# Half of the guard to GpSimd, and the second norm's end one unit later, in a four-layer decoder

## The chip, the core and the metric

The kernel runs on one core of a Trainium2 chip. The core has five engines that work through their own instruction queues in order and meet only at semaphores: TensorE (PE in the profile, with PEld for its weight loads), VectorE (DVE), ScalarE (ACT), GpSimd (POOL) and SyncE (SP), which here issues most of the transfers. The metric is the device time of one execution in microseconds (us). Less is better.

## The reference, cut to what matters

The program is a decoder of four layers on 128 sequences of 64 positions and 128 channels. Each layer has self-attention, attention to a context of the same size, and a feed-forward part. The change touches one part alone, the second layer's attention to the context (`L1_xattn`):

```python
x = x + _L1_xattn_ref(ctx_1024, _layernorm(x, axis=-1), ...)

def _L1_xattn_ref(encoded, decoded, Wq, bq, Wk, bk, Wv, bv, gamma, beta):
    # q from decoded, k and v from encoded; 16 heads of 8 channels
    qk = jnp.einsum('bhqd,bhkd->bhqk', q, k)
    qk = jnp.where(jnp.isnan(qk), -jnp.inf, qk)
    attn = jax.nn.softmax(qk, axis=-1)
    attn = jnp.where(jnp.isnan(attn), 0.0, attn)
    v = jnp.where(jnp.isnan(v), 0.0, v)
    z = jnp.einsum('bhqk,bhkd->bhqd', attn, v)
    z = z.reshape(B, Sq, D)
    x = z + decoded
    mu = jnp.mean(x, axis=-1, keepdims=True)
    var = jnp.var(x, axis=-1, keepdims=True)
    return (x - mu) * jax.lax.rsqrt(var + LN_EPS) * gamma + beta
```

So there is a first norm (of x, before the attention) and a second norm (of attention plus the normed x), scaled by gamma, shifted by beta and then added to x. The weights that are not a number become zero: the kernel does that by a maximum with 0, which it calls the guard.

## The kernel before, in words

The activations `x` stay in the core's memory as 64 tiles of 128 rows. Four tiles make a **group** (512 rows), so there are 16 groups. An attention part goes through its groups in halves of two tiles, called **units**; unit u belongs to group u // 2. `chain` (from L251 on) writes the order of all work of a layer's attention parts out by hand: the second layer's chain has 32 groups, 16 of the self-attention and then 16 of the attention to the context, and each engine executes its instructions in the order in which `chain` emits them.

In unit u the chain emits, in this order: the hooks of place "a"; `maxima` of unit u + 1 (scores in PE, four DVE reductions, L555, and five small POOL instructions that split the maxima into three bf16 pieces, L561 to L565); the second `mix` of the unit before (PE, L671 and L680); `divide` of the unit before (ACT's logarithm and exponential, L700 and L701, and three DVE instructions, L703 to L707); the first `weights` (PE L613 and L622, then four ACT exponentials into the tile p, L648). Then an odd unit finishes the group before (PE L913, ACT L917, transfers L920), projects a later group's keys and queries (L454, L459) and measures x of a group four ahead (DVE L205 and L206, then `ve` and `rs` on POOL, L208 and L210). An even unit computes values (PE L488, DVE L502 and L503, ACT L511) and turns an input (L432, L440). Then come the first guard of the unit (L656), the hooks of place "b", the second `weights`, the first `mix`, the turning of the maxima (PE L573, DVE L577), the second guard, in an even unit the scaling of the first norm of a group three ahead (`norm_act`: two POOL instructions for `nb`, L218 and L219, and four ACT activations, L221), and the hooks of place "c".

A `mix` can't begin before the guard of its weights: it multiplies the values by p, whose first 512 columns and last 512 columns are two halves of the tile, and it needs both from its first few matmuls on.

The second norm runs in hooks, counted in units from a group's own first unit: `load` (even, "b" of unit 4) fetches z from memory by SP, L890; `add` (odd, "a" of unit 5) adds the normed x on POOL, L895; `measure` (odd, "b" of unit 5) computes the statistics on DVE and POOL; `last` (even, "c" of unit 6) calls `normed_add`, which scales z by `norm_act` and then emits three POOL instructions on 128x512: times gamma (L874), plus beta (L875), and x plus z (L877). z has two buffers.

Behind the chain the second layer's feed-forward part begins. Its first input needs the x that the last L877 writes.

Of the kernel before, what the change touches and what calls it, by code (L numbers as in the profile page):

```python
# [53 lines left out]
def bc(ap, axis, n):  # L54

    v = ap.unsqueeze(axis)
    shape = list(v.shape)
    shape[axis] = n
    return v.broadcast_to(shape)


class Decoder:
# [163 lines left out]
    def norm(self, dst, src, stats=None):  # L226
        mv, rs = self.stats(src) if stats is None else stats
        for i in range(G):
            self.nc.vector.tensor_scalar(  # L229
                out=dst[:, i, :], in0=src[:, i, :], scalar1=mv[:, i, 0:1],  # L230
                scalar2=rs[:, i : i + 1], op0=ALU.subtract, op1=ALU.mult,
            )
# [419 lines left out]
    def guard(self, q, i):  # L652
        if q["kind"] == "guarded":

            for p in q["p", i]:
                self.nc.vector.tensor_scalar_max(p, p, 0.0)  # L656

    def mix(self, u, i, q):

# [209 lines left out]
    def normed_add(self, q, gamma, beta):  # L869

        nc, g, z = self.nc, q["g"], q["z"]
        norm = self.norm_act if q.get("norm") == "act" else self.norm
        norm(z, z, q["z_stats"])
        nc.gpsimd.tensor_tensor(out=z, in0=z, in1=bc(gamma, 1, G), op=ALU.mult)  # L874
        nc.gpsimd.tensor_tensor(out=z, in0=z, in1=bc(beta, 1, G), op=ALU.add)  # L875
        xg = self.x[:, g * G : (g + 1) * G, :]
        nc.gpsimd.tensor_tensor(out=xg, in0=xg, in1=z, op=ALU.add)  # L877

    def l1_xattn(self, wp):
        nc = self.nc  # L880
        w = self.qkvo(["L1_xattn_WqT", "L1_xattn_WkT", "L1_xattn_WvT"], wp)


        heads = self.dram.tile([self.nt * 2, H, S * HD], F32, name="l1x_heads")
        rows = heads.rearrange("s h (r d) -> (s h r) d", d=P)

        def load(q):
            g = q["g"]
            q["z"] = self.zp.tile([P, G, P], F32, tag="z", name="z")
            nc.sync.dma_start(  # L890
                out=q["z"], in_=rows[g * W : (g + 1) * W, :].rearrange("(t p) d -> p t d", p=P)
            )

        def add(q):
            nc.gpsimd.tensor_tensor(out=q["z"], in0=q["z"], in1=q["xn"], op=ALU.add)  # L895

        def measure(q):
            q["z_stats"] = self.stats(q["z"])

        def last(q):  # L900
            self.normed_add(q, self.spread["L1_xattn_gamma"], self.spread["L1_xattn_beta"])

        def finish(q, cxT):
            g = q["g"]

            zh = self.zh[q["n"] % 2]
            for r in range(2):
                ps = self.place().rearrange("p (d q) -> p d q", d=4)
                for d in range(4):

                    cols = self.consts[:, 4 * r + d : 4 * r + d + P : 4]
                    for i in range(G):
                        nc.tensor.matmul(  # L913
                            ps[i * 32 : (i + 1) * 32, d, :], lhsT=cols,
                            rhs=cxT[:, i * P : (i + 1) * P], start=True, stop=True,
                        )
                nc.scalar.copy(zh[:, :, 4 * r : 4 * r + 4], ps.rearrange("h d q -> h q d"))  # L917
            for i in range(G):
                k = 2 * (g * G + i)
                nc.sync.dma_start(  # L920
                    out=heads[k : k + 2].rearrange("s h n -> h s n"),
                    in_=zh[i * 32 : (i + 1) * 32 : 2].rearrange("h (s q) d -> h s (q d)", s=2),
                )

        return dict(
            hooks={
                ("b", 4): load, ("a", 5): add, ("b", 5): measure, ("c", 6): last,
            },
            w=w, source="ctx", finish=finish, bq=self.vec["L1_xattn_bq"],
            bk=self.vec["L1_xattn_bk"], bv3=self.row3["L1_xattn_bv"], kind="guarded", scale=1.0,  # L930
            norm="act",
        )
# [1300 lines left out]
```

## Time and profile before

| What | us |
|---|---|
| median of three runs | 3945.98 (3937.51 to 3946.89) |
| the profiled execution's own time | 3928.93 |
| its span, from the first to the last instruction | 3926.8 |
| PE busy in the span | 3279.9 (84%) |
| DVE busy | 2639.9 (67%) |
| ACT busy | 1924.3 (49%) |
| POOL busy | 1918.9 (49%) |
| L656 on DVE, 128 instructions, first and last start | 1263.5 and 1571.8 |
| L874, L875 and L877 on POOL in this part, each | 1.26 to 1.45 |

The span has many stages with different limits, so the shares above are averages. The stage of the change is a stretch of 309 us, 1263.5 to 1572.8, of which PE is busy 263.4, DVE 246.4, ACT 198.3 and POOL 154.4 us. In a line of the trace in order of time the first number is the start in us from the span's start, the second the duration (of several alike, from the first's start to the last's end), then follow engine, line, operation, output and inputs, shapes and count; in brackets stands the idle time before it and who ended it. A line of waits names who waited, for whom, how long in total, how often, and the longest.

### The profile page before, as it was taken

Reading aid. Unit: us, or ns where it says so; the run is one execution under the profiler, and the core shown is the slowest. Engines: PE = TensorE matmul, PEld = TensorE weight load, DVE = VectorE, ACT = ScalarE, POOL = GpSimd, SP = SyncE. Lnnn points to the kernel's source line nnn. Section 1 sums busy time; section 2 is a strip of 40 time slices with the busy share of each in tenths; the row PEclk is TensorE's granted clock in tenths of the full one; section 3 lists DMA queues with packets and bytes.
Section 4 is the critical chain, followed back from the end, with each engine's and each line's share of the span. In section 5 each row is a group of like instructions: output and inputs, shape, how many; then the busy total and the mean of one; then the engine's idle time right before and its main releaser. Section 6 shows DMA issues by size and latency. Waiting matters only on the chain.

```text
span 3926.8 us, 174155 instructions
## 1 busy us (share of the span) xinstructions
PE 3279.9 (84%) x76225; PEld 2164.2 (55%) x76237; DVE 2639.9 (67%) x7604; ACT 1924.3 (49%) x4720; POOL 1918.9 (49%) x3087
## 2 busy tenths in 40 slices
PE   5999996645999888467999998498896998799898
PEld 4666663323666666234666775244444666566566
DVE  6776675644887788696667766344435677898675
ACT  3566773103555666585556664122233555456422
POOL 3334664685442455684223434267775436863221
PEclk9999997656999999558999998699998999999999
DMA  3222222443111221000112222133333211111111
GB/s 99 65 65 79 85 95 58 101 90 70 58 55 42 64 68 57 22 1 29 53 56 71 102 93 59 37 63 74 72 65 76 69 54 52 42 44 56 54 46 36
DMA packets 246815, 243.20 MB, mean 62 GB/s; under 512 B 58459, under 2 KB 166883, under 8 KB 246054
## 3 DMA queue, kind: packets, MB, share of 16 engines
q1 hardware_dynamic: 137014, 165.24, 12.9%
q0 software_dynamic: 35264, 29.54, 5.2%
q10 hardware_dynamic: 73776, 37.27, 3.3%
q8 instruction: 599, 9.81, 1.1%
q14 instruction: 162, 1.33, 0.1%
HBM read 97.57 MB, written 63.04 MB: 41 GB/s over the span
## 4 chain that ended last, share of the span: by engine, by line
PE 57%; DVE 18%; POOL 10%; issue 6%; ACT 5%; DMA 4%; SPq 1%; another core or an unknown queue 0%; ACTq 0%; POOLq 0%; DVEq 0%
PE ps L613 6%; PE ps L540 6%; PE po L671 6%; PE po L680 5%; PE ps L454 4%; DVE m L555 3%; PE ps L722 3%; PE ps L2055 2%; PE ps L488 2%; PE pg L2036 2%; PE pu L2040 2%; DVE xn L229 2%; POOL rs L210 2%; PE ps L432 1%; DVE sb L549 1%
## 5 line engine op out<-in xcount | busy, mean ns | idle before, releaser
L648 ACT ACTIVATE p<-ps 128x256 f32<-128x256 f32 x2048 | 620.2, 391 | 152.7 <-PE ps L622 143.8
L555 DVE TENSOR_REDUCE m<-ps 128x8 f32<-128x512 f32 x896 | 555.9, 682 | 185.4 <-PE ps L540 183.0
L561 POOL CAST mx<-m 128x32 bf16<-128x32 f32 x256 | 56.0, 219 | 920.0 <-DVE m L555 919.6
L671 PE MATMUL po<-p,vx 128*32 128x64 f32 x18432 | 411.9, 224 | 86.8 <-DVE p L656 40.7
L613 PE MATMUL ps<-qx,kT 32*64 32x128 f32 x18432 | 430.3, 283 | 15.0 <-issue 9.2
L671 PEld LDWEIGHTS po<-p,vx 128*32 128x32 f32 x18432 | 302.4, 110 | 243.0 <-issue 116.4
L613 PEld LDWEIGHTS ps<-qx,kT 32*64 32x64 f32 x18432 | 277.7, 132 | 178.8 <-issue 99.9
L1287 POOL DMA_INDIRECT l_rows_y<-y,l_idx x192 | 306.5, 1596 | 130.2 <-DVE y L2071 57.1
L680 PE MATMUL po<-p,consts 128*32 128x128 f32 x8192 | 341.4, 276 | 9.5 <-issue 9.0
L540 PE MATMUL ps<-kx,qT 32*64 32x256 f32 x8192 | 308.6, 393 | 7.9 <-DMA kx<-kT 4.1
L700 ACT ACTIVATE r<-po 128x256 f32<-128x256 f32 x224 | 85.8, 383 | 416.5 <-PE po L680 407.1
L1280 POOL DMA_INDIRECT xe<-l_rows_n,l_idx x192 | 204.8, 1066 | 124.1 <-issue 40.6
L210 POOL TENSOR_TENSOR rs<-ve,neghalf 128x4 f32<-128x4 f32 x240 | 252.0, 1050 | 19.9
L577 DVE COPY mT<-ps 128x256 bf16<-128x256 bf16 x256 | 73.3, 286 | 243.6 <-PE ps L573 242.8
L680 PEld LDWEIGHTS po<-p,consts 128*32 128x32 f32 x8192 | 221.1, 111 | 16.4 <-issue 15.4
L540 PEld LDWEIGHTS ps<-kx,qT 32*64 32x64 f32 x8192 | 162.4, 133 | 83.3 <-issue 40.5
L208 POOL TENSOR_SCALAR ve<-mv 128x4 f32<-128x4 f32 x240 | 57.5, 240 | 308.3 <-DVE mv L206 294.1
L206 DVE BATCH_NORM_AGGREGATE mv<-st 128x2 f32<-128x6 f32 x960 | 172.5, 181 | 31.2
L205 DVE BATCH_NORM_STATS2 st<-x 128x6 f32<-128x128 f32 x704 | 186.7, 265 | 4.3 <-POOL x L329 4.0
L2045 DVE SCALAR_TENSOR_TENSOR hT<-pu,ub,sg 128x512 f32<-128x512 f32 x128 | 95.8, 750 | 138.3 <-PE pu L2040 101.0
L622 PE MATMUL ps<-mT,pick 32*64 32x128 bf16 x8192 | 179.2, 216 | 9.4 <-issue 9.4
L511 ACT COPY vx<-ps 64x512 f32<-64x512 f32 x256 | 149.0, 582 | 29.4 <-PE ps L488 15.2
(398 smaller groups left out, 7496.9 us busy)
## 6 DMA issues: line engine op xcount, KB each, us to landing
qx<-qT SPq DMA_DIRECT2D x560, 64.0 KB
kx<-kT SPq DMA_DIRECT2D x512, 64.0 KB
l_rows_y<-zeros SPq DMA_DIRECT2D x64, 256.0 KB
cT<-in_ctxT SPq DMA_DIRECT2D x64, 256.0 KB
fed<-l_rows_y ACTq DMA_DIRECT2D x64, 256.0 KB
l_rows_n<-fn ACTq DMA_DIRECT2D x32, 256.0 KB
l_turned<-fT ACTq DMA_DIRECT2D x32, 256.0 KB
s_xT<-l_turned SPq DMA_DIRECT2D x32, 256.0 KB
```

The source lines that it names most:

```text
L205: nc.vector.bn_stats(st[:, i, :], src[:, i, :])
L206: nc.vector.bn_aggr(mv[:, i, :], st[:, i, :])
L210: nc.gpsimd.tensor_tensor(out=rs, in0=ve, in1=self.neghalf, op=ALU.pow)
L540: nc.tensor.matmul(ps[r][s * S : (s + 1) * S, i * 256 : (i + 1) * 256], lhsT=qT[f, k], rhs=kx[f, :, k], start=mask != "causal", stop=mask ...
L555: nc.vector.tensor_reduce(m[:, :, r, :], ps[r].rearrange("p (t h k) -> p t h k", t=2, k=S), AX.X, ALU.max)
L613: nc.tensor.matmul(heads(r, o)[:, :, s, :], lhsT=kT[f, k], rhs=qx[f, o:4:2, k], start=s == 0 and mask is None, stop=s == 1 and not softmax,)
L622: nc.tensor.matmul(st[r][o * S : (o + 1) * S, j * P : (j + 1) * P], lhsT=self.pick[f, 2 * j + o, :], rhs=q["mT"][f, i, :], start=False, st ...
L648: nc.scalar.activation(p[:, 2 * r : 2 * r + 2], st[r], AF.Exp, scale=1.0 if mask == "bias" else scale)
L671: nc.tensor.matmul(po[e * 32 : (e + 1) * 32, 0, i, s * S : (s + 1) * S], lhsT=vx[:, k, j, :], rhs=p[j // 4][:, j % 4, s * S : (s + 1) * S] ...
L680: nc.tensor.matmul(po[e * 32 : (e + 1) * 32, 1, i, :], lhsT=self.spread_sum[:, jp, :], rhs=p[e // 2][:, (2 * e + jp) % 4, :], start=jp == ...
L1280: self.nc.gpsimd.indirect_dma_start(out=dst, out_offset=None, in_=table, in_offset=bass.IndirectOffsetOnAxis(ap=idx, axis=0), bounds_check ...
L1287: self.nc.gpsimd.indirect_dma_start(out=table, out_offset=bass.IndirectOffsetOnAxis(ap=idx, axis=0), in_=src, in_offset=None, bounds_check ...
```

## The change

Two things change, both in the second layer's attention to the context. First, of each guard's two instructions the second goes to GpSimd: the first 512 columns of p are guarded on VectorE, the last 512 on GpSimd. Second, `normed_add` no longer calls `norm_act` where that is the norm; a hook `scale` does so at the old place ("c" of unit 6), and the rest, times gamma, plus beta and the addition to x, is emitted by a hook `later` in "b" of unit 7. The hooks of a place are emitted for the older group first, so `later` of one group stands ahead of `measure` of the next. The last of the 16 groups keeps the old place for all of it. The reach of the hooks, `far` in the chain, becomes 7.

```diff
     def guard(self, q, i):
         if q["kind"] == "guarded":
 
-            for p in q["p", i]:
-                self.nc.vector.tensor_scalar_max(p, p, 0.0)
+            for engine, p in zip((self.nc.vector, self.nc.gpsimd), q["p", i]):
+                engine.tensor_scalar_max(p, p, 0.0)
...
     def normed_add(self, q, gamma, beta):
 
         nc, g, z = self.nc, q["g"], q["z"]
-        norm = self.norm_act if q.get("norm") == "act" else self.norm
-        norm(z, z, q["z_stats"])
+        if q.get("norm") != "act":
+            self.norm(z, z, q["z_stats"])
         nc.gpsimd.tensor_tensor(out=z, in0=z, in1=bc(gamma, 1, G), op=ALU.mult)
...
         def measure(q):
             q["z_stats"] = self.stats(q["z"])
+
+        def scale(q):
+            self.norm_act(q["z"], q["z"], q["z_stats"])
+            if q["g"] == self.ng - 1:
+                last(q)
+
+        def later(q):
+            if q["g"] < self.ng - 1:
+                last(q)
 
         def last(q):
             self.normed_add(q, self.spread["L1_xattn_gamma"], self.spread["L1_xattn_beta"])
...
             hooks={
-                ("b", 4): load, ("a", 5): add, ("b", 5): measure, ("c", 6): last,
+                ("b", 4): load, ("a", 5): add, ("b", 5): measure, ("c", 6): scale, ("b", 7): later,
             },
```

## The prediction

> **What bounds the kernel now.** I began with the page's first lines, to see how large the stage is that the change touches.
>
> ```profile
> span 3926.8 us, 174155 instructions
> ...
> L1140 POOL TENSOR_SCALAR hq<-h x64: 1917/1918/1982, 1621.4 to 1798.7; 128x512 bf16<-128x512 f32 x64
> ...
> L1382 POOL TENSOR_SCALAR ex<-ex x16: 404/404/458, 370.4 to 651.4; 128x256 f32<-128x256 f32 x16
> ...
> L656 DVE TENSOR_SCALAR p<-p x128: 392/420/1497, 1263.5 to 1571.8; 128x512 f32<-128x512 f32 x128
> ```
>
> The last three lines come from asking for single source lines (shortest, median, longest ns). The guard runs from 1263.5 to 1572 us, so only 309 us of the span change, and the tail behind them. Next, the engines' busy time by stretch: us, then PE, PEld, DVE, ACT, POOL busy.
>
> ```profile
> 1267.00:1323.80 56.80, 52.13 (x1754) 37.58 (x1750) 46.35 (x116) 38.43 (x100) 17.08 (x47) 1.00 0.21 64
> 1323.80:1511.20 187.40, 157.12 (x5034) 111.40 (x5027) 149.27 (x379) 119.62 (x317) 101.28 (x198) 0.96 0.22 67
> ```
>
> The first stretch holds three groups, before any second norm's scale and addition runs; the second holds nine with it: 18.9 us against 20.8 us for a group (two units). Nothing is full in the second, PE 84%, DVE 80%. So a circle of waits sets the pace. The waits on PE in that stretch:
>
> ```profile
> PE po L671 <- DVE p L656: 27.7, 25, 3.2
> PEld po L671 <- DVE p L656: 39.2, 51, 3.3
> ```
>
> PE waits for the guard. Then one 20.0 us group in order of time, engine by engine.
>
> ```profile
> 1405.61 1.65 ACT L221 ACTIVATE xn<-x,nb,rs 128x128 f32<-128x128 f32 x4
> 1407.16 1.63 ACT L221 ACTIVATE z<-z,nb,rs 128x128 f32<-128x128 f32 x4
> 1408.70 0.45 ACT L700 ACTIVATE r<-po,tiny 128x256 f32<-128x256 f32 x1
> ...
> 1411.73 1.27 POOL L877 TENSOR_TENSOR x<-x,z 128x512 f32<-128x512 f32 x1
> 1412.96 1.45 POOL L895 TENSOR_TENSOR z<-z,xn 128x512 f32<-128x512 f32 x1
> 1414.36 0.40 POOL L561 CAST mx<-m 128x32 bf16<-128x32 f32 x1
> ...
> 1416.06 0.23 POOL L208 TENSOR_SCALAR ve<-mv 128x4 f32<-128x4 f32 x1
> ...
> 1412.39 0.18 DVE L206 BATCH_NORM_AGGREGATE mv<-st 128x2 f32<-128x6 f32 x1
> 1412.49 2.20 DVE L656 TENSOR_SCALAR p<-p 128x512 f32<-128x512 f32 x2
> 1416.56 0.75 DVE L656 TENSOR_SCALAR p<-p 128x512 f32<-128x512 f32 x2
> ...
> 1414.74 0.58 PE L671 MATMUL po<-p,vx 128*32 128x64 f32 x26 [1.10 <-DVE p L656]
> 1416.03 0.28 PE L573 MATMUL ps<-identh,mx 128*128 128x128 bf16 x2 [0.21 <-POOL mx L565]
> 1417.29 0.66 PE L671 MATMUL po<-p,vx 128*32 128x64 f32 x30
> ```
>
> The three additions of the previous group (L874, L875, L877, 4.1 us, waiting for ACT's scale) and L895 stand on POOL ahead of the maxima's pieces (L561 to L565). They also lie beside the odd unit's first guard, which takes 2.20 us for two instructions, where it takes 0.75 us at 1416.56. Two marks divide the group: **t**, DVE's end of measuring x in the odd unit (1412.57), and **s**, the start of PE's second mix of that unit (1417.29). Now t to s is 4.72 us, and s to the next t 15.28 us (1397.29 to 1412.57).
>
> **The change, part by part.** *Removed from DVE:* 64 of 128 guards. Undisturbed they cost 0.39 us, so 1.5 us of DVE a group.
>
> *Added to POOL:* 64 guards of a form that the trace doesn't hold (128x512, f32 in place, max). L1382 takes 404 ns for 256 columns and L219 238 ns for 4, thus 0.66 ns a column, and 0.58 us for 512. L1140 has the full size, and a min, but a bf16 output and two operations: 1.92 us. These are the ends. The GPSIMD Engine Reference, section 3.1, gives 769 ns for 512 elements of a tight loop; by that, an estimate, I would add 51 us below instead of 42. I take 0.58 us, since L1382 is nearer in kind (f32 to f32 with a scalar), and keep 1.92 us for the range.
>
> *Moved:* the three POOL additions go from the end of the even unit to the odd unit, behind its first guard and ahead of its second. They carry no DMA. `scale` keeps its place (four ACT activations, two POOL multiplications for nb). SP's load of z into the buffer that they free (L890, issued at 1422.1) comes some 9.5 us after t, and they now end near t+6.5: no wait on SP, and nothing behind it. POOL's order in the odd unit becomes L895, the maxima's pieces, ve and rs of x, half a guard, three additions, ve and rs of z, half a guard.
>
> *From t to s, new.* ve and rs follow the measuring, beside DVE's half guard; at 1309.05 the same pair ended 1.8 us later. Half guard 0.65 with its gap; three additions 4.1 (1408.88 to 1413.00); ve and rs of z 1.4 (1416.06 to 1417.38, with the gap); half guard 0.65. Sum **8.6 us**, against 4.72. PE could be there at t+4.8 (1.8 + 0.65 to start the first mix, then 2.34 of mix, turning and maxima: 1414.74 to 1417.29 less its 0.21 wait). So the second half guard holds PE for 3.8 us. DVE's own half is done by then, even if an addition delays it: late without cost.
>
> *From s to the next t, new.* DVE's reductions are over when PE starts, so the division starts when ACT has r, at s+2.15 instead of s+2.53, and the even unit gains 0.45 us up to ACT's weights (ready at s+7.85, not 8.3). POOL's half guard ends at s+8.5. Behind it now stand the nb multiplications, which before were done at 1402.4; xn starts at s+9.0 instead of 8.32, z follows, and L700 starts at s+12.1 instead of 11.41. Then r 0.95, division 1.35, measuring 1.65: the next t at s+**16.1**. The maxima's pieces no longer stand behind the additions, which saves PE's 0.21 us wait and the doubled guard; both are in these figures. All in all 24.7 us a group against 20.8: **+3.9**, nine times **+35**.
>
> *The last four groups* measure no x and, after the first, scale no xn. Without these, r is ready near s+11.5, p(U) at 12.7, and 0.65 + 4.1 + 1.4 + 0.65 make 19.5 us a group. The gaps between ACT's L700 of the even units are 18.5, 17.8, 19.0, then 7.0 us for the last odd unit; I get 19.5, 19.5, 19.5 and 10.2: **+6.5**.
>
> *The first three groups* have no additions. The odd unit's half guard waits for ve and rs (t+2.45 instead of t+0.73); PE loses about 1.5 us, the even unit gives 0.2 back: **+4**.
>
> *The tail.* After PE's last mix (1573.25) POOL goes through three groups' norms; one takes 10.7 us (L895 at 1579.88 and 1590.56), and the last addition ends at 1603.15. With the additions behind the next group's L895, they cover ACT's scale and DVE's statistics. The last z lands near 1587; then 1.3 + 4 + 1.4 + 0.5 + 1.7 + 4 = 12.9, and 2.6 for the next layer's factors that lie between: near 1600, **-3**.
>
> *Sum.* 35 + 6.5 + 4 - 3 = **+42 us**. The profiled execution took 3928.93 us (span 3926.8 and 2.1 around it), and would take 3971; it lies 17 us under the median shown, 3945.98, to which the same sum gives **3988 us**.
>
> *The rule on the shared port.* L656's longest is 1497 ns where its shortest is 392, beside POOL's additions. SBUF — State Buffer, Who interferes with whom, says that VectorE's fast two-port operations and GpSimd hold a common port pair exclusively: one fully blocks. By the row, a half guard on DVE loses up to 1.1 us a time; by the rule it could wait for all three additions (4 us, to t+6.5), and the reductions behind it end near t+9, while the division needs them at t+10.75. Either way the sum stays. The rule speaks against handing guards to POOL while DVE guards too, but the delay is POOL's order, not the port.
>
> **The rivals.** *The slow guard*: POOL's max costs 1.92 us, as L1140's min. The circle holds three half guards, so +1.34 x 3 = +4 on each of 13 groups, 7 more in the first three: near **4047**. For it: L1140 has the shape. Against it: its bf16 output, and L1382.
>
> *Half recovered*: the chain from t to s is as above, but the next unit recovers half of the delay, since ACT and DVE have room. Then about +2 on each of 9 groups, +4 elsewhere, -3: near **3965**. Against it: after s everything waits for PE's mix.
>
> *Faster*: taking the additions out of the way of the maxima's pieces is worth more than the new waits. Its place is the odd unit. If the second half guard came in time (t to s under 3.9 us, when s to t takes 16.1), groups would run as without additions, 18.9 us: -1.9 x 9, -3 in the tail, some +6 elsewhere: near **3932**. The point that decides is POOL's work between the two guards, 5.5 us by its rows, against 2.3 us that PE has to do there. It speaks against this rival that even a guard at no cost leaves t to s at 7.3.
>
> *No change*: the new wait and the removed one cancel, if PE's need of the second guard came some 3 us later.
>
> **How the numbers follow.** Likeliest, 0.62: 3988, by itself 3970 to 4008. Slow guard 0.22: 4047, with 10 us of error either way. Half recovered 0.06; faster 0.06; no change 0.04. The range leaves out faster, no change, and the upper part of the slow guard: **3962 to 4052**. A measurement of this kernel can tell about 0.3%, 12 us, from no change. Faster 0.06, same 0.05 (the fourth, with a bit of half recovered), slower 0.89.
>
> **What would show it.** POOL's guard rows: 64, near 0.6 us (or 1.9). PE's wait before L671 for POOL's p, some 3.8 us in each odd unit with additions. ACT waiting for nb ahead of xn. L874 no longer waiting for ACT's z, and after the odd unit's first guard. Odd units' DVE guards without 1.1 us blocks at the first guard. Groups of 24 to 25 us from the fourth to the twelfth. I am wrong if the second guard stands ahead of the additions on POOL, or groups stay at 20 us.

## The result, and the profile after

The changed kernel takes 4038.35 us (median of four runs, 4037.40 to 4042.02), beside 3941.89 us for the kernel before (3937.51 to 3946.89): a ratio of **1.0246**, interval 1.0230 to 1.0263. It is slower by 96 us, and the forecast was 42. Its profiled execution took 4042.02 us, with a span of 4040.2.

First the guard's two halves, each source line asked for by itself (shortest, median and longest ns, then the first and last start in us):

```profile
L656 POOL TENSOR_SCALAR p<-p x64: 1479/1488/1626, 1274.6 to 1681.6; 128x512 f32<-128x512 f32 x64
L656 DVE TENSOR_SCALAR p<-p x64: 394/420/1302, 1275.7 to 1677.0; 128x512 f32<-128x512 f32 x64
```

The half guard costs **1.49 us** on GpSimd; the prediction put 0.58 into its sum. Next the changed kernel's busy time by stretch (start and end, length, PE, PEld, DVE, ACT and POOL busy with their instructions, granted clock, the transfers' share, GB/s): the first groups without additions, then the nine groups with them, then the last four.

```profile
1282.40:1349.60 67.20, 52.88 (x1665) 37.62 (x1664) 39.12 (x99) 36.37 (x97) 35.37 (x64) 0.95 0.18 54
1349.60:1605.60 256.00, 190.45 (x5039) 131.87 (x5039) 126.46 (x343) 119.88 (x317) 149.34 (x234) 0.82 0.16 49
1605.60:1685.20 79.60, 56.13 (x1751) 41.39 (x1744) 40.05 (x97) 36.77 (x101) 53.34 (x71) 0.86 0.15 43
```

The nine groups take 256 us, 28.4 each, where they took 187.4, 20.8 each. Two numbers differ from the same stretch of before at once: POOL is busy 149 us instead of 101, and TensorE's granted clock is **0.82** instead of 0.96. PE does the same work, 5039 matmuls against 5034, in 190 us instead of 157. The waits in these nine groups, in total us, number and longest:

```profile
POOL p L656 <- ACT p L648: 60.4, 18, 4.1
PEld po L671 <- POOL p L656: 56.6, 27, 3.3
...
PE po L671 <- POOL p L656: 51.7, 27, 3.0
...
ACT xn L221 <- POOL nb L219: 18.7, 9, 2.1
...
PE po L671 <- DVE p L656: 13.0, 19, 1.0
```

PE now waits 27 times, three times a group, for POOL's half. One odd unit in order of time, POOL, DVE, PE and then ACT:

```profile
1440.24 1.50 POOL L656 TENSOR_SCALAR p<-p 128x512 f32<-128x512 f32 x1
1441.70 1.27 POOL L874 TENSOR_TENSOR z<-z,spread 128x512 f32<-128x512 f32 x1
1443.06 1.26 POOL L875 TENSOR_TENSOR z<-z,spread 128x512 f32<-128x512 f32 x1
1444.39 1.44 POOL L877 TENSOR_TENSOR x<-x,z 128x512 f32<-128x512 f32 x1
...
1447.12 1.50 POOL L656 TENSOR_SCALAR p<-p 128x512 f32<-128x512 f32 x1
...
1438.55 0.18 DVE L206 BATCH_NORM_AGGREGATE mv<-st 128x2 f32<-128x6 f32 x1
1438.65 0.41 DVE L656 TENSOR_SCALAR p<-p 128x512 f32<-128x512 f32 x1
...
1441.79 0.96 PE L671 MATMUL po<-p,vx 128*32 128x64 f32 x26 [2.37 <-POOL p L656]
...
1448.67 0.96 PE L671 MATMUL po<-p,vx 128*32 128x64 f32 x26 [2.90 <-POOL p L656]
...
1450.64 0.47 ACT L700 ACTIVATE r<-po,tiny 128x256 f32<-128x256 f32 x1 [10.57 <-PE po L680]
```

With the prediction's two marks: t is 1438.73, where the last L206 on x ends, and s is 1448.67, the second mix. That is 9.94 us, before 4.72. The next t is at 1466.71, so s to t is 18.04, before 15.28. The order is the one foreseen: half guard, three additions without a wait ahead of them, the norm's `ve` and `rs`, half guard, mix. But each half guard is 1.5 us, and the 26 matmuls behind a wait take 0.96 us where they took 0.58 at 1414.74 in the kernel before.

To add it all up I use ACT's logarithm L700 as a milestone: the last one ahead of the first guarded unit, the even units' that bound the nine groups, and the last of all (us).

| | first groups | nine groups | last four | sum |
|---|---|---|---|---|
| before | 64.3 | 187.4 | 62.2 | 314.0 |
| after | 78.0 | 256.0 | 79.6 | 413.6 |
| difference | +13.7 | +68.6 | +17.3 | +99.6 |
| predicted | +4 | +35 | +6.5 | +45.5 |

From the last L700 to the next layer's first norm it is 27.9 us (1685.15 to 1713.04), before 29.8 (1573.41 to 1603.18): -1.9, predicted -3. Together that is +97.7, beside 96.5 between the medians. The profiled spans differ by 113, but 12 of that lie ahead of the first guarded unit, where both kernels do the same, so these are not counted.

### The profile page after: what moved, and what is told of

Same layout as the page of the kernel before. It is cut to its first block, busy times and chain, and to the rows that moved or that the text cites. A ratio compares the mean times of both kernels' runs of the same rounds, so it can differ in the third digit from the quotient of the medians.

```text
span 4040.2 us, 174206 instructions
## 1 busy us (share of the span) xinstructions
PE 3332.8 (82%) x76237; PEld 2197.6 (54%) x76237; DVE 2606.0 (65%) x7540; ACT 1924.1 (48%) x4720; POOL 2001.9 (50%) x3151
## 4 chain that ended last, share of the span: by engine, by line
PE 58%; DVE 15%; POOL 11%; issue 6%; ACT 5%; DMA 4%; SPq 1%; ACTq 0%; DVEq 0%; POOLq 0%
PE ps L613 7%; PE po L671 6%; PE ps L540 6%; PE po L680 5%; PE ps L454 4%; PE ps L488 3%; PE ps L722 3%; PE ps L2064 3%; PE pg L2045 2%; PE pu L2049 2%; DVE m L555 2%; POOL rs L210 2%; POOL p L656 2%; DVE xn L229 1%; PE ps L622 1%
## 5 line engine op out<-in xcount | busy, mean ns | idle before, releaser
L671 PE MATMUL po<-p,vx 128*32 128x64 f32 x18432 | 425.1, 226 | 157.5 <-POOL p L656 81.3
L671 PEld LDWEIGHTS po<-p,vx 128*32 128x32 f32 x18432 | 310.5, 112 | 320.2 <-issue 132.4
L613 PE MATMUL ps<-qx,kT 32*64 32x128 f32 x18432 | 440.8, 287 | 19.5 <-issue 13.8
L613 PEld LDWEIGHTS ps<-qx,kT 32*64 32x64 f32 x18432 | 285.0, 134 | 186.4 <-issue 108.2
L680 PE MATMUL po<-p,consts 128*32 128x128 f32 x8192 | 352.5, 281 | 9.9 <-issue 9.4
L540 PE MATMUL ps<-kx,qT 32*64 32x256 f32 x8192 | 318.2, 401 | 7.3 <-DMA kx<-kT 4.6
L700 ACT ACTIVATE r<-po 128x256 f32<-128x256 f32 x224 | 85.8, 383 | 428.6 <-PE po L680 416.4
L703 DVE TENSOR_TENSOR e<-po,r 128x256 f32<-128x256 f32 x256 | 106.8, 417 | 147.5 <-ACT r L701 134.6
L622 PE MATMUL ps<-mT,pick 32*64 32x128 bf16 x8192 | 184.8, 219 | 12.4 <-issue 12.2
L206 DVE BATCH_NORM_AGGREGATE mv<-st 128x2 f32<-128x6 f32 x960 | 172.4, 181 | 31.2
## 6 DMA issues: line engine op xcount, KB each, us to landing
l_rows_y<-zeros SPq DMA_DIRECT2D x64, 256.0 KB
cT<-in_ctxT SPq DMA_DIRECT2D x64, 256.0 KB
fed<-l_rows_y ACTq DMA_DIRECT2D x64, 256.0 KB
l_rows_n<-fn ACTq DMA_DIRECT2D x32, 256.0 KB
l_turned<-fT ACTq DMA_DIRECT2D x32, 256.0 KB
s_xT<-l_turned SPq DMA_DIRECT2D x32, 256.0 KB
```

Source lines behind the costliest of these rows:

```text
L206: nc.vector.bn_aggr(mv[:, i, :], st[:, i, :])
L540: nc.tensor.matmul(ps[r][s * S : (s + 1) * S, i * 256 : (i + 1) * 256], lhsT=qT[f, k], rhs=kx[f, :, k], start=mask != "causal", stop=mask ...
L613: nc.tensor.matmul(heads(r, o)[:, :, s, :], lhsT=kT[f, k], rhs=qx[f, o:4:2, k], start=s == 0 and mask is None, stop=s == 1 and not softmax,)
L622: nc.tensor.matmul(st[r][o * S : (o + 1) * S, j * P : (j + 1) * P], lhsT=self.pick[f, 2 * j + o, :], rhs=q["mT"][f, i, :], start=False, st ...
L671: nc.tensor.matmul(po[e * 32 : (e + 1) * 32, 0, i, s * S : (s + 1) * S], lhsT=vx[:, k, j, :], rhs=p[j // 4][:, j % 4, s * S : (s + 1) * S] ...
L680: nc.tensor.matmul(po[e * 32 : (e + 1) * 32, 1, i, :], lhsT=self.spread_sum[:, jp, :], rhs=p[e // 2][:, (2 * e + jp) % 4, :], start=jp == ...
```

## The experiments

The theory is **price**: the order of waits is as predicted, but GpSimd's half guard is two and a half times as long as assumed. Rivals are **order** (the additions' new place ahead of the second guard makes most of the loss), **queue** (POOL is the wrong place at any price) and **clock** (TensorE's granted clock falls because of the waits). The table after the last experiment gives each kernel's stretches.

### Each part alone

The guard's split in the kernel before, with the additions in their old place:

```diff
 # the kernel before
-            for p in q["p", i]:
-                self.nc.vector.tensor_scalar_max(p, p, 0.0)
+            for engine, p in zip((self.nc.vector, self.nc.gpsimd), q["p", i]):
+                engine.tensor_scalar_max(p, p, 0.0)
```

> The guard's split alone; the second norm's end stays in the even unit. Theory 'order' (GpSimd's queue and its 1.49 us guard set the group's length, and where the three additions stand decides how much): the additions now precede the odd unit's two half guards, together some 26 us a group for nine groups instead of 20.8, first three groups as in the changed kernel (+14), last four about +12: near 4015. Rival 'price' (the guard's 1.49 us is the whole loss and the move is harmless or helps): as slow as the changed kernel or slower, 4038 or more.

Measured: 4036.97 us against 3942.74, ratio 1.0234 (1.0218 to 1.0250): +94. Then the move alone, both halves on VectorE:

```diff
 # the changed kernel
-            for engine, p in zip((self.nc.vector, self.nc.gpsimd), q["p", i]):
-                engine.tensor_scalar_max(p, p, 0.0)
+            for p in q["p", i]:
+                self.nc.vector.tensor_scalar_max(p, p, 0.0)
```

> The move alone; both halves are guarded on VectorE. Theory 'order': without a guard on GpSimd nothing on TensorE's path stands behind the additions; the first odd guard is freed of them and the second one lies beside them instead, so groups stay near 20 us and the tail gains 2: 3930 to 3945, the same as before. Rival 'port' (the additions beside the second guard block it for all three of them, 4 us): near 3965. Rival 'price': faster than before by up to 0.4%.

Measured: 3929.41 us, ratio 0.9967 (0.9952 to 0.9981): 13 us **faster** than the kernel before. So the split makes the whole loss, in either order, and the move by itself gains. Why the split costs as much without the move is seen in POOL's and PE's rows of the split alone:

```profile
1460.60 1.27 POOL L874 TENSOR_TENSOR z<-z,spread 128x512 f32<-128x512 f32 x1 [2.83 <-ACT z L221]
...
1464.67 1.45 POOL L895 TENSOR_TENSOR z<-z,xn 128x512 f32<-128x512 f32 x1
...
1468.91 1.50 POOL L656 TENSOR_SCALAR p<-p 128x512 f32<-128x512 f32 x1
...
1470.46 0.96 PE L671 MATMUL po<-p,vx 128*32 128x64 f32 x26 [5.11 <-POOL p L656]
```

There the additions stand ahead of the odd unit's first half guard instead of its second: PE waits 5.11 us at once. A half guard on POOL is behind the additions in both orders. In the move alone nothing on PE's way is behind them but a blocked guard:

```profile
1423.20 0.73 DVE L656 TENSOR_SCALAR p<-p 128x512 f32<-128x512 f32 x2
...
1425.06 1.27 POOL L874 TENSOR_TENSOR z<-z,spread 128x512 f32<-128x512 f32 x1
1425.62 2.40 DVE L656 TENSOR_SCALAR p<-p 128x512 f32<-128x512 f32 x2
...
1428.08 0.58 PE L671 MATMUL po<-p,vx 128*32 128x64 f32 x26 [1.10 <-DVE p L656]
```

Two halves on VectorE take 0.73 us free and 2.40 beside L874 and L875, and the wait has moved from the first guard of the odd unit to the second. The gain comes as -5.0 us in nine groups, -4.0 in the last four and -2.1 in the tail (27.7 us where it took 29.8).

### The order: the additions behind the second guard

```diff
 # the changed kernel
-                ("b", 4): load, ("a", 5): add, ("b", 5): measure, ("c", 6): scale, ("b", 7): later,
+                ("b", 4): load, ("a", 5): add, ("b", 5): measure, ("c", 6): scale, ("c", 7): later,
```

> The changed kernel with the three additions emitted behind the odd unit's second guard (place c instead of b of unit 7). Theory 'order': t to s falls from 9.9 to some 6.4 us, the even unit's guards wait longer for GpSimd, groups of 23 to 24 us: near 3986. Rival 'price': 4038 as the changed kernel, since GpSimd does the same work.

Measured: 4002.35 us, ratio 1.0146 (1.0131 to 1.0161). In between: the order is worth 36 us of the 96, and 60 stay without it. POOL's rows, then PE's first mix:

```profile
1477.38 1.50 POOL L656 TENSOR_SCALAR p<-p 128x512 f32<-128x512 f32 x1
...
1480.17 1.50 POOL L656 TENSOR_SCALAR p<-p 128x512 f32<-128x512 f32 x1
1481.63 1.43 POOL L874 TENSOR_TENSOR z<-z,spread 128x512 f32<-128x512 f32 x1
...
1478.93 0.96 PE L671 MATMUL po<-p,vx 128*32 128x64 f32 x26 [2.38 <-POOL p L656]
```

The second half guard now starts 2.8 us after the first, not 6.9 after it, and t to s falls to 7.2 us (1475.87 to 1483.05). But PE still waits 2.38 us for the first, since `ve` and `rs` and 1.5 us of guard lie between the measuring and the mix, and a group is 24.5 us. Neither theory has it alone: with a half guard of the same price, its place behind the additions decides how long PE waits for it.

With both halves on VectorE the same place was also tried:

```diff
 # the changed kernel, both halves on VectorE as above
-                ("b", 4): load, ("a", 5): add, ("b", 5): measure, ("c", 6): scale, ("b", 7): later,
+                ("b", 4): load, ("a", 5): add, ("b", 5): measure, ("c", 6): scale, ("c", 7): later,
```

> The move alone, both halves guarded on VectorE, and the three additions one place further: behind the odd unit's second guard (place c of unit 7), as in the fourth run. Theory 'order': no guard lies beside an addition any more, t to s falls from 4.7 to some 3.3 us, of which the additions take back up to 0.8 us from the next unit's division, whose second instruction reads two tiles: groups near 19.3 us against 20.0 in the second run, 3920 to 3930. Rival: the maxima's pieces, now behind the additions in the even unit, come too late for TensorE's turning, or the division waits for all three additions: no better than the second run, 3930 or more.

Measured: 3945.65 against 3949.34, ratio 0.9988 (0.9974 to 1.0002): no difference that can be told. A miss: I expected a gain.

### What sets the price

A multiplication by one in place of the maximum, to see whether the maximum is dear:

```diff
 # the changed kernel
-            for engine, p in zip((self.nc.vector, self.nc.gpsimd), q["p", i]):
-                engine.tensor_scalar_max(p, p, 0.0)
+            a, b = q["p", i]
+            self.nc.vector.tensor_scalar_max(a, a, 0.0)
+            self.nc.gpsimd.tensor_scalar_mul(b, b, 1.0)
```

> The changed kernel with GpSimd's maximum replaced by a multiplication by 1.0 on the same half tile (that half isn't guarded; the queue's order is unchanged). If the price is the maximum's, the instruction takes near 0.6 us and the time is that of the prediction's sum with the clock's loss on top, 3988 to 4000. If the price is that of any such instruction on 128x512 f32, it takes 1.49 us again and the time stays at 4038.

Measured: 4041.66, ratio 1.0256 (1.0239 to 1.0273), and the row is `1487/1488/1624` ns. So it isn't the maximum that is dear: a lone multiplication of this size costs the same. Then why did L1382, the row I extrapolated from, take 404 ns for 256 columns? It multiplies and adds in one instruction. A kernel that gives the groups eight forms in turn tells them apart:

```diff
 # the changed kernel: GpSimd's half b, form = group % 8
...
+            if form == 0:
+                gp.tensor_scalar(out=b, in0=b, scalar1=1.0, scalar2=0.0, op0=ALU.mult, op1=ALU.add)
+            elif form == 1:
+                gp.tensor_scalar(out=b, in0=b, scalar1=0.0, scalar2=0.0, op0=ALU.max, op1=ALU.add)
...
+            elif form == 3:
+                for j in range(2):
+                    gp.tensor_scalar_max(b[:, 2 * j : 2 * j + 2], b[:, 2 * j : 2 * j + 2], 0.0)
...
+            elif form == 5:
+                gp.tensor_scalar_add(b, b, 0.0)
...
+            else:
+                for j in range(4):
+                    gp.tensor_scalar_max(b[:, j], b[:, j], 0.0)
```

> The changed kernel with eight forms of GpSimd's instruction on the half tile, by the group's number: multiply by 1 and add 0 in one instruction; maximum and add; maximum and multiply; the maximum in two halves of 256 columns; maximum and minimum; add 0 alone; subtract and minimum; the maximum in four quarters (the forms without a maximum leave that half unguarded). Theory 'pair' (the trace's 404 ns for 256 columns belong to multiply-and-add as a pair): the first form takes near 0.6 us, single operations 1.5, pairs with a minimum 1.9 as in the feed-forward part. Rival 'size' (256 columns are cheap, 512 not): the first form takes 1.5 us or more, and each half of 256 columns near 0.4.

Measured (one execution, 4054.7 us), by source line: multiplication and addition together, addition alone, the maximum on 256 and on 128 columns:

```profile
L659 POOL TENSOR_SCALAR p<-p x8: 620/621/622, 1272.3 to 1505.2; 128x512 f32<-128x512 f32 x8
...
L670 POOL TENSOR_SCALAR p<-p x8: 1492/1498/1511, 1396.0 to 1642.6; 128x512 f32<-128x512 f32 x8
...
L666 POOL TENSOR_SCALAR p<-p x16: 838/853/1035, 1339.0 to 1593.5; 128x256 f32<-128x256 f32 x16
...
L677 POOL TENSOR_SCALAR p<-p x32: 519/526/730, 1453.8 to 1689.7; 128x128 f32<-128x128 f32 x32
```

The pair of a multiplication and an addition costs 0.62 us, a lone addition 1.50. The four other pairs that were tried, each with a maximum or a minimum in it, had medians of 1.92 to 1.93, as L1140 had. A lone maximum takes some 2.5 ns a column and 0.2 us besides: 0.53, 0.85 and 1.49 us for 128, 256 and 512. The extrapolation of 0.58 us was right to 0.04 us, for a form that isn't the guard's.

### The prediction's price under the prediction's sum

The cheap pair put in everywhere, all else as in the changed kernel:

```diff
 # the changed kernel
-            for engine, p in zip((self.nc.vector, self.nc.gpsimd), q["p", i]):
-                engine.tensor_scalar_max(p, p, 0.0)
+            a, b = q["p", i]
+            self.nc.vector.tensor_scalar_max(a, a, 0.0)
+            self.nc.gpsimd.tensor_scalar(
+                out=b, in0=b, scalar1=1.0, scalar2=0.0, op0=ALU.mult, op1=ALU.add
+            )
```

> The changed kernel with GpSimd's operation on its half made a multiplication by one and an addition of zero in one instruction (0.62 us in the study of forms, against 1.49), so that this half is not guarded; all else, order included, as in the changed kernel. It puts the prediction's own price back under the prediction's own sum. Theory 'price' (only the size of the half guard was wrong in the prediction): 24.8 us a group or a little more, about 40 us over the kernel before, 3975 to 3998 us beside a kernel before at 3945. Rival 'queue' (GpSimd is a bad place for it at any price that is over DVE's 0.4, because of what stands ahead of it there): over 4015. Rival 'clock' (the waits lower TensorE's clock even when short): granted clock under 0.88 in the nine groups and over 26 us a group.

Measured: 4015.00 against 3956.37 (this chip's kernel before), ratio 1.0148 (1.0133 to 1.0164): **+59**, not about 40: more than *price* gave (+30 to +53 over its 3945) and less than *queue* (over +70). The price alone doesn't close the gap: it takes 38 of the 96 us away, and 17 us more than the forecast 42 remain. Rows of two groups in order of time: PE's s and what follows it, DVE's t, PE's next s:

```profile
1430.18 0.58 PE L674 MATMUL po<-p,vx 128*32 128x64 f32 x26 [2.06 <-POOL p L657]
...
1431.19 1.00 PE L613 MATMUL ps<-qx,kT 32*64 32x128 f32 x32
...
1432.72 1.98 PE L488 MATMUL ps<-L_xattn_WvT_sb,cT 128*64 128x64 f32 x32
...
1447.18 0.18 DVE L206 BATCH_NORM_AGGREGATE mv<-st 128x2 f32<-128x6 f32 x1
...
1455.78 0.96 PE L674 MATMUL po<-p,vx 128*32 128x64 f32 x26 [2.96 <-POOL p L657]
```

The first s is 1430.18, t is 1447.36, the next s is 1455.78. So t to s is 8.42 us, where the prediction worked out 8.6, and s to t is 17.18, where it worked out 16.1. The missing microsecond a group is in the second, and the rows show where: behind s, L613 takes 1.00 us and L488 1.98, while the granted clock of these nine groups is 0.90. In the kernel before, behind its s at 1417.29, the same work took 0.69 and 1.15:

```profile
1418.37 0.69 PE L613 MATMUL ps<-qx,kT 32*64 32x128 f32 x32
...
1419.35 1.15 PE L488 MATMUL ps<-L_xattn_WvT_sb,cT 128*64 128x64 f32 x32
```

ACT's second weights of the even unit, which everything up to the next t hangs on, are then ready at s+8.99 (1439.17) instead of the s+7.85 of the prediction. These 1.14 us are 0.31 and 0.83 from L613 and L488.

The same at a real guard of that price: GpSimd guards the last 128 columns alone.

```diff
 # the changed kernel
-            for engine, p in zip((self.nc.vector, self.nc.gpsimd), q["p", i]):
-                engine.tensor_scalar_max(p, p, 0.0)
+            a, b = q["p", i]
+            self.nc.vector.tensor_scalar_max(a, a, 0.0)
+            self.nc.vector.tensor_scalar_max(b[:, 0:3], b[:, 0:3], 0.0)
+            self.nc.gpsimd.tensor_scalar_max(b[:, 3], b[:, 3], 0.0)
```

> The changed kernel with GpSimd's part cut to the last of the tile's eight columns of 128 (0.53 us in the study of forms); VectorE guards the other seven in two instructions, so every weight is guarded. Theory 'price': as the kernel with the cheap form, within 10 us of it, so the size of the half guard is what counts and not what it computes. If VectorE's third instruction a unit counts, up to 10 us more than that. Rival 'queue': over 4015.

Measured: 4006.89, ratio 1.0122 (1.0108 to 1.0137), within 10 us of the cheap pair. What counts here is how long POOL takes, not what it computes. *Queue* keeps its share too: at 0.53 and 0.62 us, little over VectorE's 0.42, a guard part on POOL costs 50 and 59 us, where the same order with both halves on VectorE gained 13.

### The clock

The guards and their order stay as they are, and TensorE is given more to do ahead of them: for odd units the scores of the second weights are computed three times more, and those of the maxima two times more, into the same place. In PE's order both stand just ahead of a mix that waits.

```diff
 # the changed kernel, in the scores of maxima and of the second weights
+        busy = q["kind"] == "guarded" and u % 2 == 1
-        for i in range(2):
+        for i in [0, 1] * (3 if busy else 1):
...
+        busy = q["kind"] == "guarded" and u % 2 == 1 and i == 1
+        passes = 4 if busy else 1
-        for s in range(2):
+        for n, s in [(n, s) for n in range(passes) for s in range(2)]:
...
```

> The changed kernel with more work for TensorE where it waits: in the odd units of this part the score matmuls of the second weights are done four times and those of the maxima three times (32 matmuls each, the same values written again). Theory 'clock' (TensorE's granted clock falls after the waits for GpSimd's half guards, and the mix behind them runs slower, some 1 us a group): the clock of the nine groups rises from 0.82 towards 0.95, groups fall from 28.4 to 27.4 us, near 4025 in spite of more work. Rival: the slow matmuls have another cause, or the clock doesn't matter where GpSimd sets the pace: 4038 or more, by up to 30 if the repeated matmuls come late.

Measured: 4039.54 against 3949.34, ratio 1.0236 (1.0211 to 1.0261), +90: hardly any of the total. The stretch of nine groups says more, a window and then three rows of it:

```profile
1352.80:1595.30 242.50, 194.20 (x6469) 141.38 (x6461) 130.59 (x343) 120.06 (x316) 149.37 (x234) 0.96 0.17 52
```

```profile
1446.48 0.58 PE L675 MATMUL po<-p,vx 128*32 128x64 f32 x26 [2.50 <-POOL p L660]
...
1448.47 1.15 PE L488 MATMUL ps<-L_xattn_WvT_sb,cT 128*64 128x64 f32 x32
...
1453.02 1.22 ACT L652 ACTIVATE p<-ps 128x256 f32<-128x256 f32 x4
```

The wait of the second mix is still 2.50 us, where it was 2.90 (all 27 together 41.2, where they were 51.7), but the granted clock is 0.96, the matmuls behind the wait take 0.58 us, L488 takes 1.15, and ACT's weights are ready at s+7.76 (prediction: 7.85). The nine groups take 242.5 us with 1430 matmuls **more** than the changed kernel's, 13.5 us less. In the first groups, where the changed kernel's clock was 0.95 anyway, the added matmuls cost 6 us (84.2 against 78.0); so little of the total is left. So a wait of 2.50 us did not in itself bring the clock down: with the added work ahead of it the clock stayed at 0.96, without it the stretch had 0.82.

### The move alone, again

Both versions with VectorE guarding all, beside the two of the section before the last:

> The later scale and addition with both halves guarded by VectorE, run again beside the other three. If the gain of the first run is real: 0.995 to 0.998 of the kernel before.

> The same with the additions behind the second guard, run again beside the other three. First run: 0.9988, no difference that can be told, though its stage was 4 us shorter. If its place is as good as the other's: within 0.1% of it; if the clock takes it back: 0.2 to 0.3% above it.

Measured, against 3956.37: additions ahead of the second guard 3944.82, ratio **0.9969** (0.9956 to 0.9981); behind it 3945.45, 0.9976 (0.9966 to 0.9986). The first gain is repeated to 0.0002. This time both places beat the kernel before, by 12 and 11 us, and the two can't be told apart.

All stretches, by the milestones of the first table (us), with the mean of a group of the nine and their granted clock:

| | first | nine | last four | a group | clock |
|---|---|---|---|---|---|
| before | 64.3 | 187.4 | 62.2 | 20.8 | 0.96 |
| after | 78.0 | 256.0 | 79.6 | 28.4 | 0.82 |
| split alone | 80.8 | 247.2 | 82.2 | 27.5 | 0.88 |
| move alone, first and second time | 64.1, 64.7 | 182.4, 182.4 | 58.2, 58.6 | 20.3 | 0.98 |
| move alone, additions behind the guard, first and second time | 63.7, 63.9 | 177.6, 177.3 | 59.6, 62.8 | 19.7 | 0.95 |
| after, additions behind the guard | 78.1 | 220.4 | 69.0 | 24.5 | 0.91 |
| after, times one | 81.0 | 259.6 | 80.0 | 28.8 | 0.82 |
| after, cheap pair | 71.8 | 231.2 | 69.7 | 25.7 | 0.90 |
| after, 128 columns | 71.7 | 228.0 | 68.1 | 25.3 | 0.89 |
| after, TensorE kept busy | 84.2 | 242.5 | 79.0 | 26.9 | 0.96 |

The table shows why the place behind the guard gained no more than the place ahead of it. Its nine groups are 5 us shorter, but the last four are 1 to 4 us longer, and the tail, from the last L700 to the next layer's first norm, is 4 to 6 us longer: 33.8 and 31.8 us, beside 27.7 and 28.0. In the tail of the second run POOL waits 1.81 us (to 1580.42) and 2.19 us (to 1592.08) for DVE's statistics, with the additions behind these waits; ahead of the guard the same additions fill them.

## Why the prediction was right in its kind and wrong in its size

The step that failed is the cost of "64 guards of a form that the trace doesn't hold": **0.58 us taken, 1.49 measured**. The row chosen was the nearest in type, but not in operation: L1382 is a multiplication with an addition, the only one of the forms tried here that is cheap. Both ends of the range had been named, and the choice of the near one was the error. The guard lies between them: neither L1382 nor L1140 (a subtraction with a minimum, 1.92 us) is a single operation. The outcome falls to the rival of the slow guard (4047), in part by luck: its price is 0.43 us too high, and that stands in for the clock, which it didn't have either. The Trainium skill's GPSIMD Engine Reference, section 3.1, with its 769 ns for 512 elements of a loop, lies on the wrong side too: the trace has 1488 for this instruction.

What the right price makes of the sum, by the prediction's own steps: the circle holds three half guards, so 0.91 x 3 = 2.7 us more on each group. The marks of the groups shown, in us (the means of all nine stand in the table above):

| | t to s | s to t | group |
|---|---|---|---|
| predicted at 0.58 | 8.6 | 16.1 | 24.7 |
| measured with the cheap pair (0.62) | 8.42 | 17.18 | 25.6 |
| predicted, worked out again at 1.49 | 10.4 | 17.0 | 27.4 |
| measured, after | 9.94 | 18.04 | 28.0 |
| measured, TensorE kept busy (1.49) | 9.88 | 16.81 | 26.7 |

- **Nine groups**, +35: with 2.7 us a group more, +59.6; measured +68.6. The other 9 us are the balance of two terms. The clock, which no step of the prediction has, costs 13.5 us, by the nine groups with TensorE kept busy (242.5 against 256.0). And t to s is half a microsecond a group shorter than worked out again. With TensorE kept busy s to t is within 0.2 us of the predicted step; without, 1.0 over it, at either price.
- **The last four**, +6.5: with 2.7 each +17.4, measured +17.3. With the cheap pair it was +7.5.
- **The first groups**, +4: 2.7 on three groups makes +12.2, measured +13.7; with the cheap pair +7.4. Here the step was also 3 us too small at its own price.
- **The tail**, -3: measured -1.9. The mechanism is there, and the last z landed when foreseen: the last L895 starts at 1698.62 after 4.92 us of waiting for it, 13.5 us behind the last L700; predicted was 13.6 (1587 and 1573.41). The error is in the adding up: 1587, 12.9 and 2.6 make 1602.5, which is -0.6 and not -3. In the trace the rest takes 14.4 us (1698.62 to 1713.01), not 15.5.

Together that is 35 + 6.5 + 4 - 3 = 42 from the prediction, 44 from the price and some 12 from the clock and the first groups: the 97.7 measured. The cheap pair checks the middle term. From 1.49 to 0.62 us the same rule, three times 0.87 us on each of 16 groups, gives 42 us; the three stretches of the table fall by 41 (413.6 to 372.6).

The prediction also set a group worked out from one of 20.0 us beside the mean of 20.8. That did no harm: the groups of 21 and the first one of 23.7 us that raise this mean have no counterpart with the cheap pair, whose groups take 25.5 to 26.6.

What was right: the order of POOL's queue, L874 straight behind the first half guard without a wait for ACT's z, ACT waiting 2.1 us for `nb` ahead of xn nine times, DVE's half done long before PE's wait ends. "Some 3.8 us" of wait in an odd unit came as two, 2.37 and 2.90, since the first half guard is late too. The **shared port** decided nothing in the change, as said: in the cheap pair's kernel a half guard on DVE beside the additions took 1.27 us instead of 0.42, over at 1452.46, and PE's wait for POOL's half ended only at 1455.78.

Of the rivals, **half recovered** fell: from s on nothing of the delay was made up for, s to t got longer and not shorter. **Faster** was right about its mechanism and wrong about its place in this change: moving the additions gains 12 to 13 us, but only where no guard stands behind them on POOL. Its size was overrated too: 0.5 us a group, not 1.9, because VectorE's second guard of the odd unit is now the blocked one (2.40 us, above).

What stays open: what sets how far the granted clock falls, and why the first groups lost 7.4 us at the cheap price where 4 were foreseen.

## What to carry to other kernels

Before work is handed to another engine, price it by a row of the same engine with the same operation, not just the same type and size; where there is none, the ends of the range deserve near equal chances, or better, a small run that measures the instruction alone. A step that lies three times on the circle of waits multiplies its error by three. And when a change makes TensorE wait in short stretches, look at the granted clock as a term of its own: the matmuls behind the wait, not only the wait, get longer.

## What the runs showed of the hardware

- **GpSimd's tensor-with-scalar instruction** (128x512, f32 in place): a multiplication and an addition 0.62 us, any single operation tried (maximum, multiplication, addition) 1.49 to 1.50, a pair with a maximum or minimum 1.92 to 1.93. So two operations can be cheaper than one.
- **VectorE beside GpSimd**: two half guards 0.73 us free, 2.40 beside two POOL instructions of 1.3 us (L874, L875); a single one 0.42 and 1.27.
- **The clock** fell in the changed kernel, where two waits of 2 to 3 us in each odd unit have short work between them. After the 2.90 us wait at 1448.67 PE's rows are slow up to 1452.04, then L488 is back at 1.15: 3.4 us. The Trainium skill's TensorE: Matmul & The Clock Gate, Part 1, gives about 3.4 us of sustained work for the full clock to come back, which fits; its idle window, also 3.4 us, would by itself have left the clock alone here, as no wait of these nine groups was longer than 3.3. The measurement decides: 0.82. Nor does the longest wait order the kernels: the longest matmul wait of the nine groups is 3.2 us in the kernel before, with a clock of 0.96, 5.1 in the split alone, with 0.88, and 1.6 with the 128 columns, with 0.89.
